# Group norms' deviation by ScalarE's logarithm and exponential in place of VectorE and GpSimd's power

## The chip, the cores and the metric

The kernel runs on one core of a Trainium2 chip. The metric is the device time of one execution in microseconds; the time of a kernel is the median of its runs. The engines are named as the profile names them: PE (TensorE's matmuls), PEld (its weight loads), DVE (VectorE), ACT (ScalarE), POOL (GpSimd) and SP (SyncE, which issues DMAs).

## The reference

Four layers work on 16 images of 192 channels and 32 x 32 pixels, all in fp32. Each layer is a residual around a block that sees the group-normalised image:

```python
def _gn(v, G=32, eps=1e-5):
    B_, C_, H_, W_ = v.shape
    g = v.reshape(B_, G, C_ // G, H_, W_)
    m = jnp.mean(g, axis=(2, 3, 4), keepdims=True)
    s = jnp.var(g, axis=(2, 3, 4), keepdims=True)
    return ((g - m) / jnp.sqrt(s + eps)).reshape(v.shape)

x = x + _L0_conv_ref(_gn(x), ...)   # layer norm, up projection, mLSTM over 1024 tokens, 3x3 conv, batch norm
x = x + _L1_conv_ref(_gn(x), ...)   # layer norm, selective scan (16 states, 384 channels), projection
x = x + _L2_conv_ref(_gn(x), ...)   # depthwise 3x3 conv, batch norm
x = x + _L3_conv_ref(_gn(x), ...)   # projection, depthwise conv, four selective scans, layer norm, router
return x
```

What matters here is `1 / sqrt(s + eps)` in `_gn`: one number for each of 32 groups, in each of 16 images and four layers.

## The kernel before, in words

An image lies in SBUF as 96 partitions x 2 halves of the channels x 1024 pixels. A group of six channels is six neighbouring partitions, so `group_norm` takes each partition's mean and variance on DVE (`bn_stats` L351, `bn_aggr` L352), averages over the six partitions with a small matmul against the constant `group` (L355, PSUM tile `mm`), builds the second moment on DVE (`gnmean` L357, `gnd` L359, `gnq` L361 and L362), and averages that with a second matmul (L365). The result in PSUM is the variance of the group, two columns for the two halves of the channels. DVE adds eps while it moves it to the SBUF tile `gnr` (L367), and `pow_mhalf` raises that in place to the power of -0.5 on GpSimd (L309). The caller then normalises the two halves on DVE, each a `tensor_scalar` over 96 x 1024 that reads `gnmean` and `gnr`:

- L543 in `layer0_image` (layer 0, 16 images), which `layer0_front`'s layer norm reads with the matmul L377;
- L1240 in `layer1_front` (layer 1), read likewise by L377;
- L1351 in `layer1_tail` (the norm ahead of layer 2), which fills `xpad`, sent to DRAM by L1356;
- L1545 in `layer3_front` (layer 3), which fills `xpad` too. There `router` also reads `gnr` on DVE (L1680).

The kernel runs in three stages: layer 0, then layers 1 and 2 together, then layer 3. Each has a main chain, and beside it tasks that a small planner (`Side`) interleaves: a task is a Python generator, added with a start and an end in units of main steps, and at each tick the planner draws as many of its pieces as are due. `group_norm` is part of such tasks (`image`, `front`, `tail`). The order in which instructions are written is then handed to the tile framework, which schedules each engine's queue by its own estimates and inserts the semaphores; instructions of one engine run in the order of its queue.

In layer 0 the main chain works through chunks of 128 tokens (`layer0_step`). GpSimd adds the mask and the row to the decay matrix `e`, 128 x 1536 (L705, L706), scales `hs` by `mhv` (L841), forms `vr` (L755) and adds `ht` (L857); ACT takes the exponential of `e` (L711); ACT takes a logarithm and an exponential of the small tile `mhv` (L839, L840); DVE multiplies `ht` (L854) ahead of L543.

In layers 1 to 3 the main chain is a selective scan (`scan_run`): per state n and unit of 512 tokens, ACT scales `xbt` (three L966) and forms the decay `da` (L986, five buffers) for each of three channel tiles, PE turns `xbt` into the PSUM tile `xb` (L994, and L997 with the diagonal made by GpSimd's L976), DVE scans (L1010, `h`), GpSimd copies the carry (L1016) and multiplies `h` by the row `cb` (L1017, 128 x 1536), and PE adds the result up in PSUM (L1028). ACT and PE work one to two steps ahead of the scan.

`layer_norm` already forms its deviation with AF.Ln and AF.Exp (L386, L387). Silu needs another table of ACT; after each Silu the kernel loads the set `natural_log_exp_and_others` again (L598, L1284). `batch_norm` and `layer3_weights` also call `pow_mhalf`; they are not touched.

Of the kernel before, what the change touches and what calls it, by code (L numbers as in the profile page):

```python
# [11 lines left out]
AF = mybir.ActivationFunctionType  # L12
# [4 lines left out]
ADD, SUB, MUL, MAX, MIN, POW = ALU.add, ALU.subtract, ALU.mult, ALU.max, ALU.min, ALU.pow  # L17

C = 192
HP = 96  # L20
# [8 lines left out]
EPS = 1e-5  # L29
# [160 lines left out]
def halves(n=S, step=512):  # L190
    return [slice(i, i + step) for i in range(0, n, step)]
# [83 lines left out]
class Program:  # L275
# [68 lines left out]
    def group_norm(self, pool, psum, x):  # L344

        nc = self.nc
        st = pool.tile([HP, 2, 2, 6], F32, name="gnst")
        mv = pool.tile([HP, 2, 2], F32, name="gnmv")
        for m in range(2):
            for i, h in enumerate(halves()):  # L350
                nc.vector.bn_stats(st[:, m, i], x[:, m, h])  # L351
            nc.vector.bn_aggr(mv[:, m], st[:, m].rearrange("p a b -> p (a b)"))  # L352
            yield 1
        ps = psum.tile([128, 512], F32, name="mm")
        nc.tensor.matmul(ps[:HP, :2], self.k("group", HP), mv[:, :, 0], start=True, stop=True)  # L355
        mean = pool.tile([HP, 2], F32, name="gnmean")
        nc.vector.tensor_copy(mean, ps[:HP, :2])  # L357
        d = pool.tile([HP, 2], F32, name="gnd")
        nc.vector.tensor_tensor(d, mv[:, :, 0], mean, SUB)  # L359
        q = pool.tile([HP, 2], F32, name="gnq")  # L360
        nc.vector.tensor_tensor(q, d, d, MUL)  # L361
        nc.vector.tensor_tensor(q, q, mv[:, :, 1], ADD)  # L362
        yield 1
        ps = psum.tile([128, 512], F32, name="mm")
        nc.tensor.matmul(ps[:HP, :2], self.k("group", HP), q, start=True, stop=True)  # L365
        r = pool.tile([HP, 2], F32, name="gnr")
        nc.vector.tensor_scalar(r, ps[:HP, :2], EPS, None, ADD)  # L367
        self.pow_mhalf(r)
        yield 1
        return mean, r, d  # L370

# [1339 lines left out]
```

## Time and profile before

| What | Value |
|---|---|
| Median of three runs | 17368.59 us (17350.56 to 17390.61) |
| Profiled execution | 17403.5 us, span 17401.7 us |
| Mean granted clock of TensorE | 0.951 |
| GpSimd's product L1017 | 2560 times, 3469 ns |
| DVE's scan L1010 | 7680 times, 1202 to 1262 ns |
| ACT's decay L986 and scaling L966 | 7680 times each, 714 and 603 ns |
| DVE's normalisations (96 x 1024) | 128 times, 0.79 us at least, 4.70 us at most |

The profile is of one execution, which has its own time; the table gives it beside its span, which runs from the first instruction to the last. In the profile's lines `out<-in` names tiles, `x` counts instructions, and a bracket or "idle before" gives the time in which the engine stood idle ahead of an instruction and what ended it. In the answers on a tile, three durations are the smallest, the median and the largest in ns; indented lines give idle time in us and how often. In the timeline the first column is the start in us from the span's start and the second how long the row took.

### The profile page before, as it was taken

How to read it: one execution, taken by the hardware profiler on the slowest of the kernel's cores; microseconds unless marked ns; L12 is line 12 of the kernel's file. 1: busy time of each engine (PE TensorE's matmuls, PEld its weight loads, DVE VectorE, ACT ScalarE, POOL GpSimd, SP SyncE). 2: the span in 40 equal slices, each digit the busy share in tenths (PEclk: the TensorE clock that was granted, in tenths of full speed). 3: DMA queues.
4: the chain of work that ended last, by engine and by line, in shares of the span. 5: the costliest groups of instructions: out<-in, count | busy, mean ns of one | idle time of the engine just before them, and what ended most of it. 6: DMA issues, size and time to landing. Idle time of an engine off the chain costs nothing. (4 is left out here: it accounts for less than half of the span.)

```text
span 17401.7 us, 263068 instructions
## 1 busy us (share of the span) xinstructions
PE 15749.6 (91%) x99452; PEld 11013.2 (63%) x99452; DVE 13122.0 (75%) x14859; ACT 11873.6 (68%) x19637; POOL 11450.8 (66%) x5555
## 2 busy tenths in 40 slices
PE   8998988888988899979899999999999999999998
PEld 4444444435555555547777777777777777777777
DVE  4444444437777777749889888888888888888888
ACT  3222322327666666648888888888888888888888
POOL 3333333425555555538788788888878888888888
PEclk8889998989999999989999999999999999999999
DMA  1111111123333343433333333323333333333332
GB/s 51 42 40 44 44 43 44 47 63 107 114 110 110 113 118 116 118 99 103 90 99 107 93 96 101 107 83 99 107 98 92 99 108 88 96 105 102 88 98 67
DMA packets 890141, 1544.65 MB, mean 89 GB/s; under 512 B 83472, under 2 KB 314653, under 8 KB 879530
## 3 DMA queue, kind: packets, MB, share of 16 engines
q1 hardware_dynamic: 888874, 1527.81, 30.3%
q8 instruction: 788, 12.91, 0.3%
q14 instruction: 479, 3.92, 0.1%
HBM read 1284.22 MB, written 243.27 MB: 88 GB/s over the span
## 5 line engine op out<-in xcount | busy, mean ns | idle before, releaser
L1017 POOL TENSOR_TENSOR h<-h,cb 128x1536 f32<-128x1536 f32 x2560 | 8872.8, 3469 | 1432.0 <-DVE h L1010 902.9
L986 ACT ACTIVATE da<-dt,neg_a 128x512 f32<-128x512 f32 x7680 | 5267.0, 714 | 1752.0 <-DVE h L1010 1687.3
L1010 DVE TENSOR_TENSOR_SCAN h<-da,carry,xb 128x512 f32<-128x512 f32 x3840 | 4652.4, 1262 | 657.1 <-PE xb L997 596.2
L1028 PE MATMUL y<-const,h 128*128 128x128 f32 x30720 | 4717.9, 276 | 128.3 <-DVE ysum L1468 54.0
L1010 DVE TENSOR_TENSOR_SCAN h<-da,xb 128x512 f32<-128x512 f32 x3840 | 4440.6, 1202 | 388.7 <-PE xb L997 270.7
L994 PE MATMUL xb<-const,xbt 128*128 128x128 f32 x23040 | 4074.6, 282 | 422.5 <-DVE h L1010 269.3
L966 ACT ACTIVATE xbt<-ut,bt 128x384 f32<-128x384 f32 x7680 | 4174.4, 603 | 246.4 <-PE xb L994 244.3
L994 PEld LDWEIGHTS xb<-const,xbt 128*128 128x128 f32 x23040 | 2757.2, 143 | 1815.5 <-issue 643.8
L1028 PEld LDWEIGHTS y<-const,h 128*128 128x128 f32 x30720 | 3684.9, 143 | 322.8 <-issue 265.4
L997 PE MATMUL xb<-diag,ut 128*128 128x128 f32 x15360 | 3016.4, 279 | 0.0
L997 PEld LDWEIGHTS xb<-diag,ut 128*128 128x128 f32 x15360 | 2383.5, 195 | 63.1 <-issue 63.1
L830 POOL TENSOR_TENSOR hs<-h,mhm 128x384 f32<-128x384 f32 x128 | 108.5, 848 | 1685.1 <-DVE den L835 1290.5
L1016 POOL COPY carry<-h 128x3 f32<-128x3 f32 x1280 | 250.5, 196 | 1220.1 <-DVE h L1010 964.7
L976 POOL TENSOR_TENSOR diag<-const,bt 128x512 f32<-128x512 f32 x640 | 680.8, 1064 | 550.5 <-PE xb L997 362.1
L705 POOL TENSOR_TENSOR e<-e,const 128x1536 f32<-128x1536 f32 x128 | 439.9, 3437 | 288.9 <-DMA e<-row 273.0
L520 PE MATMUL conv<-ya,w_conv 128*64 128x512 f32 (+1 forms) x1152 | 543.9, 656 | 66.1 <-DMA ya<-yrows 62.2
L916 PE MATMUL mm<-dbl,w_dt 45*128 45x512 f32 x960 | 532.8, 639 | 33.6 <-DVE v L1490 16.2
L711 ACT ACTIVATE e<-e 128x1536 f32<-128x1536 f32 x128 | 189.7, 1482 | 417.7 <-POOL e L706 417.4
L854 DVE TENSOR_TENSOR ht<-sz,mm 128x384 f32<-128x384 f32 x128 | 70.7, 552 | 519.5 <-PE mm L851 519.5
L1171 PE MATMUL mm<-rep,t_dw 96*32 96x512 f32 x2304 | 433.5, 614 | 23.5 <-DMA rep<-xr 17.3
L779 PEld LDWEIGHTS num<-v,p 128*128 128x128 f32 x3072 | 389.3, 201 | 102.2 <-issue 77.9
L920 DVE SCALAR_TENSOR_TENSOR dt<-lnsq,mm 128x512 f32<-128x512 f32 x480 | 322.0, 671 | 171.9 <-ACT lnsq L919 171.9
(272 smaller groups left out, 17910.1 us busy)
## 6 DMA issues: line engine op xcount, KB each, us to landing
cb<-row SPq DMA_DIRECT2D x2560, 256.0 KB
rep<-xr SPq DMA_DIRECT2D x384, 331.0 KB
e<-row SPq DMA_DIRECT2D x128, 768.0 KB
rep<-xin SPq DMA_DIRECT2D x384, 256.0 KB
rep<-xr SPq DMA_DIRECT2D x384, 228.8 KB
x<-x SPq DMA_DIRECT2D x48, 768.0 KB
xr<-xin SPq DMA_DIRECT2D x48, 612.5 KB
xr<-xpad SPq DMA_DIRECT2D x32, 867.0 KB
```

What stands on the lines that cost most here:

```text
L520: nc.tensor.matmul(o, self.w_c2[:k, t, c0 : c0 + o.shape[0]], src[:k, r0 : r0 + 16, dx : dx + W], start=t == 0, stop=t == 14, skip_group_c ...
L705: nc.gpsimd.tensor_tensor(k.e, k.e, self.k0("mask")[:, None, :].to_broadcast([128, NH, 128]), ADD)
L916: nc.tensor.matmul(ps, w_dt[:, t * 128 : (t + 1) * 128], dbl, start=True, stop=True)
L966: nc.scalar.activation(t[:, c], u.ut[:, c], AF.Copy, scale=u.bt[:, c, n : n + 1])
L976: nc.gpsimd.tensor_tensor(d, ident[:, None, :].to_broadcast([128, 4, 128]), u.bt[:, 3, n : n + 4][:, :, None].to_broadcast([128, 4, 128]), ...
L986: nc.scalar.activation(da[i, t], u.dt[:, t], AF.Exp, scale=u.neg_a(t, n))
L994: in_order(nc.tensor.transpose(xb[i, t][:, c * 128 : (c + 1) * 128], xbt[i][:, c, t * 128 : (t + 1) * 128], ident))
L997: in_order(nc.tensor.matmul(xb[i, t][:, 384:], u.ut[:, 3, t * 128 : (t + 1) * 128], u.diag[n // 4][:, n % 4], start=True, stop=True, skip_ ...
L1010: nc.vector.tensor_tensor_scan(hv, dv, xv, 0.0 if first else u.carry_in[:, n, t : t + 1], MUL, ADD)
L1017: nc.gpsimd.tensor_tensor(h[i], h[i], u.c.pop(n)[:, None, :].to_broadcast([128, 3, 512]), MUL)
L1028: in_order(nc.tensor.matmul(u.y[:, j], h[i][:, t, c * 128 : (c + 1) * 128], ident, is_transpose=True, start=n == 0 and j % 4 == 0, stop=n ...
L1171: self.nc.tensor.matmul(ps[32 * g : 32 * g + 32], blocks[:, g * side + r], seen, start=r == 0, stop=r == side - 1, skip_group_check=True,)
```

## The change

The add of eps moves into the bias of a logarithm on ACT, which reads the variance from PSUM and writes `gnr`; an exponential with scale -0.5 then forms the deviation in place, also on ACT. DVE's L367 and the call of `pow_mhalf` go.

```diff
         ps = psum.tile([128, 512], F32, name="mm")
         nc.tensor.matmul(ps[:HP, :2], self.k("group", HP), q, start=True, stop=True)
         r = pool.tile([HP, 2], F32, name="gnr")
-        nc.vector.tensor_scalar(r, ps[:HP, :2], EPS, None, ADD)
-        self.pow_mhalf(r)
+        nc.scalar.activation(r, ps[:HP, :2], AF.Ln, bias=self.k("eps", HP))
+        nc.scalar.activation(r, r, AF.Exp, scale=-0.5)
         yield 1
         return mean, r, d
```

Line numbers stay the same: in the changed kernel L367 is the logarithm and L368 the exponential. The framework schedules anew, so other instructions move a little too. In layer 0 the order stays as it was but for the first images. In layers 1 and 2 PE's, ACT's and DVE's queues have neighbours exchanged around the norms of every image: L1240 stands one scan earlier in DVE's queue, L1351 stands ahead of the scan that it followed. In layer 3 L1545 stands one scan later (a scan that followed it now precedes it), L1680 is followed by one more scan before the copy L1683, and one of SP's loads of `xtok` an image changes place. In ACT's queue the logarithm and the exponential follow L840 in layer 0, and stand among the L966 and L986 of the scan in the other layers.

## The prediction

> **What bounds the kernel now.** First the page's busy time, then the busy time by layer (layer 0; layers 1 and 2; layer 3), each row with PE, PEld, DVE, ACT, POOL and the granted clock.
>
> ```profile
> PE 15749.6 (91%) x99452; PEld 11013.2 (63%) x99452; DVE 13122.0 (75%) x14859; ACT 11873.6 (68%) x19637; POOL 11450.8 (66%) x5555
> ```
> ```profile
> 0.00:3860.00 3860.00, 3401.76 (x14460) 1725.32 (x14460) 1801.98 (x3622) 1110.81 (x1656) 1435.47 (x890) 0.88 0.18 44
> 3860.00:7660.00 3800.00, 3341.98 (x19456) 2167.84 (x19456) 2784.72 (x3055) 2508.77 (x4001) 2110.81 (x1033) 0.96 0.38 112
> 7660.00:17402.00 9742.00, 9005.87 (x65536) 7120.08 (x65536) 8535.31 (x8184) 8254.07 (x13980) 7904.54 (x3632) 0.97 0.33 97
> ```
>
> PE is near its bound everywhere, but its queue is in order, so it also stands still where it meets a late operand: 458 us in layer 0, 458 in layers 1 and 2, 736 in layer 3. The change can only win or lose inside that idle time. Next the answers for the tile gnr (first and third group below) and for the matmul L377, which reads the normalised image.
>
> ```profile
> L367 DVE TENSOR_SCALAR gnr<-mm x64: 122/145/156, 33.5 to 16416.9; 96x2 f32<-96x2 f32 x64
> L309 POOL TENSOR_TENSOR gnr<-gnr,const x64: 679/690/709, 33.7 to 16417.9; 96x2 f32<-96x2 f32 x64
> ...
>   POOL gnr L309: 95.0, 52
> ```
> ```profile
>   DVE x L543: 222.3, 45
> ...
>   DVE xf L1240: 72.3, 46
> ```
>
> The power takes 0.69 us, and VectorE sits idle 95.0 us in all for it, because it queues behind GpSimd's 3.4 us products. PE and its weight loads wait long for the normalisation itself (L543, L1240), of which the power is only the last link. Last, the timeline at one norm of each kind. Layer 0:
>
> ```profile
> 2759.37 2.75 POOL L706 TENSOR_TENSOR e<-e,uw 128x1536 f32<-128x1536 f32 x1
> 2762.08 0.69 POOL L309 TENSOR_TENSOR gnr<-gnr,const 96x2 f32<-96x2 f32 x1
> ...
> 2762.80 3.80 DVE L543 TENSOR_SCALAR x<-x,gnmean,gnr 96x1024 f32<-96x1024 f32 x2 [5.33 <-POOL gnr L309]
> ...
> 2765.93 3.73 PE L377 MATMUL mm<-x,const 96*96 96x512 f32 x4 [7.05 <-DVE x L543]
> ```
>
> Layer 1's tail (L1351) and layer 3 (L1545):
>
> ```profile
> 5226.79 0.69 POOL L309 TENSOR_TENSOR gnr<-gnr,const 96x2 f32<-96x2 f32 x1 [2.19 <-DVE gnr L367]
> ...
> 5227.82 4.64 DVE L1351 TENSOR_SCALAR xpad<-xt,gnmean,gnr 96x1024 f32<-96x1024 f32 x2
> ...
> 5228.03 3.88 POOL L1017 TENSOR_TENSOR h<-h,cb 128x1536 f32<-128x1536 f32 x1 [0.56 <-DVE h L1010]
> ```
> ```profile
> 10992.26 1.61 ACT L966 ACTIVATE xbt<-ut,bt 128x384 f32<-128x384 f32 x3
> ...
> 10995.36 0.25 PE L365 MATMUL mm<-gnq,const 96*96 96x2 f32 x2
> ...
> 10997.56 0.71 POOL L309 TENSOR_TENSOR gnr<-gnr,const 96x2 f32<-96x2 f32 x1
> ...
> 10998.31 2.24 DVE L1545 TENSOR_SCALAR xpad<-x,gnmean,gnr 96x1024 f32<-96x1024 f32 x2 [1.62 <-POOL gnr L309]
> ```
>
> A pair of normalisations takes 1.6 us alone and up to 4.64 beside a GpSimd product: who comes first at that moment matters more than the power's own 0.69 us.
>
> [...] L1351 takes 0.79 us alone and 3.94 when L1017 got in before it. [...] The trace: 204 ns for the 96x2 exponential L1690, 212 for the 128x12 logarithm L839. [...] the order of the changed kernel agrees, with 228 table loads where there were 227, the new one in the first microseconds (1.28 us).
>
> **The change part by part.** It removes 64 L367 (64 x 0.145 = 9.3 us of VectorE) and 64 powers (64 x 0.69 = 44 us of GpSimd) and adds 64 logarithms [...] and 64 exponentials (0.20): 31 us of ScalarE. None of these sums is the effect; the places are. No DMA is added; some of SP's issues swap places with a neighbour (one xtok load an image in layer 3, a few replicas in layer 1). I cost those at nothing: the loads' reader is far off.
>
> *Layer 0.* VectorE's order is unchanged but for L367, ScalarE has the pair right after L840. L711, next behind it, starts at 2762.15 and is not touched. At 2756.28 + 0.21 + 0.48 = 2757.0 the deviation is there, 5.8 us before L543 starts now. But GpSimd is in L705 and L706 until 2762.12[...]. Between L706, L841, L755 and L857 there is no gap, so the second half of L543 waits for L857 (end 2765.33) as now, 0.7 us sooner since the power is gone. L706 follows L705 after a gap of 0.08 us, and at 201.01 a half L543 slipped into just such a gap. So in the five norms of this form the first half goes at 2759.3, and half of L377 (3.73 / 2 = 1.9 us) is done before the second: 0.7 + 1.9 = 2.6 us. In nine others L706 is already running: 0.65. Sum 5 x 2.6 + 9 x 0.65 = 19 us off PE's wait; I keep three quarters, 14 us, as the next wait (for e, L711) takes some; bounds 9 and 19.
>
> *Layer 1, front (L1240), 13 steady norms.* ScalarE's logarithm stands one L966 earlier than its input allows: ScalarE waits from 5145.85 to PE's result at 5147.62, 1.8 us, with L966 (xbt) and three L986 (da) behind it. PE's tile needs that xbt at 5148.22 and gets it at 5148.5. VectorE reaches L1240 one scan (1.2 us) sooner, at 5148.85, in the middle of L1017 (to 5150.24) with L976 behind it: 2.4 us of waiting where there were 1.4, and L377 stands before the next L997 in PE's order. Worked through, the second scan after it ends at 5157.5 where it was 5157.15: a loss of 0.3 us, 4 us in all. Bounds: a gain of 1 us each (13)[...]; a loss of 2.5 (33), if PE's new order holds a scan back.
>
> *Layer 1, tail (L1351), 11 norms of the form shown.* ScalarE is idle when the matmul ends (5225.19); deviation at 5225.7. L1351 now stands ahead of the scan that releases L1017, so GpSimd is idle during both halves: 5226.57 to 5228.1, then the scan to 5229.3, where scan and pair were over at 5232.46. VectorE gains 3.1 us; PE's idle there is 1.57 <-DVE h plus 0.36 <-DVE gnr, so 1.9 us, 21 in all; I take three quarters, 16 (bounds 0, if other waits fill the place, and 3.1 x 11 = 34). L1017 comes about 1 us later; its reader is two steps off.
>
> *Layer 3 (L1545), 14 norms.* The logarithm stands between the first and second of the three L966: ScalarE waits from 10992.86 to 10995.6, 2.8 us. The third L966 ends at 10997.15 where PE asked for it at 10996.50 (0.65 us of PE, then idle anyway until 11001.73 <-DVE h); the next decay at 10997.8, its scan at 10999.9. VectorE does one scan more before L1545, arrives at 10997.7, in L976 (now from 10997.58 to 10998.62), and is done at 10999.95 where it was 11000.55 with a scan less: 1.16 + 0.6 = 1.7 us. L1680, now two scans earlier, meets L1017 sooner: about 1.2 us instead of 0.55. Net 1.0; 14 norms, less a little: 12 us. Bounds 0 and 24.
>
> Four norms with nothing beside them (the first of each layer and the last tail) go from 0.97 us between L367's start and the normalisation's to about 0.55: 1.6 us, which pays for the one table load. **Sum:** -14 + 4 - 16 - 12 = -38 us. The profiled execution took 17403.5 us (span 17401.7), 35 above the median of the three runs, so it gives 17365 for a like execution and 17330 against the median of 17368.6.
>
> **Rivals.**
> *Nothing comes of it* (17364): [...] (14 x 0.65 = 9, less L1240's 4). For it: PE at 88 to 92%. Against: PE's idle at these places is named <-DVE.
> *ScalarE's queue becomes the wait; slower.* Place: the logarithm ahead of L966 and L986 in L1240 and L1545. Price: 13 x 1.8 + 14 x 2.8 = 62 us; less layer 0's 14, 48 slower: 17417. It decides if the decays come later than the scans: they have 2.1 us to spare in layer 3 (10997.8 against 10999.9), and the five da buffers. Against: ScalarE's idle of 1752 us ahead of L986 is time in which it is ahead. For: it is 85% busy there.
> *More is gained* (17278): layer 0 19, L1351 3.1 x 11 = 34, L1545 1.7 x 14 = 24, L1240 13, sum 90.
> *It reloads tables* (each 1.28 us, 128 of them 164 us slower): excluded by the order.
>
> **Numbers.** About 0.2% (35 us) is what a measurement tells from no change. Forecast 17330: 0.50, spread on both sides of that line; nothing 0.20; more 0.12; slower 0.18. Faster 0.45, same 0.38, slower 0.17. The range goes from the larger gain (17265) to the queue's loss with a little over for the unexamined reordering of PE in layers 1 and 2 (17430).
>
> **What would show it.** VectorE's wait for gnr gone and L543's first half longer than 3.1 us in layer 0; L1351 at 0.8 us in both halves; L1545 still near 1.5 then 0.8; ScalarE idle about 2.8 us at each L367 <-PE mm L365. Wrong if L986 or L966 becomes a long releaser of PE or VectorE, if L1351 still shows 3.9, or if layer 3 is not shorter.

## The result and the profile after

The changed kernel takes 17282.36 us (median of 4 runs, 17259.77 to 17310.99) where the kernel before takes 17367.28 in the same session; the ratio is 0.9951, with a 95% interval of 0.9932 to 0.9970. That is a gain of 85 us, with an interval of 52 to 118. A second session with the same kernel gave 17266.54 against 17356.26, ratio 0.9946 (0.9933 to 0.9960). The forecast was a gain of 38 us: the direction was right, and the time lies in the range, near its faster end, but the gain is more than twice the forecast. The profiled execution took 17310.99 us (span 17309.2), which is 29 us above the median.

The page's busy time, and then the stretches of layer 0, of layers 1 and 2 and of layer 3 (duration, then PE, PEld, DVE, ACT, POOL with the number of instructions, the granted clock, the DMA share and GB/s):

```profile
PE 15753.3 (91%) x99452; PEld 11004.9 (64%) x99452; DVE 13120.8 (76%) x14795; ACT 11898.1 (69%) x19766; POOL 11425.1 (66%) x5491
```
```profile
0.00:3826.00 3826.00, 3414.34 (x14460) 1731.56 (x14460) 1819.66 (x3607) 1117.82 (x1689) 1436.29 (x874) 0.88 0.18 45
3826.00:7577.00 3751.00, 3345.51 (x19456) 2175.33 (x19456) 2757.42 (x3018) 2523.20 (x4064) 2084.65 (x1001) 0.96 0.38 114
7577.00:17310.00 9733.00, 8993.41 (x65536) 7098.04 (x65536) 8543.70 (x8171) 8257.12 (x14014) 7904.15 (x3616) 0.98 0.31 97
```

No engine's total moved by more than 26 us, and TensorE is as busy as it was (15753 us against 15750). What shrank is the time in which it stands: in layer 0 from 458 to 412 us, in layers 1 and 2 from 458 to 405. In layer 3 it is 740 where it was 736. The gain thus shows where the forecast placed 26 us in all, and does not show, in this pair of profiles, where it placed 12.

The groups of the tile gnr, and the answer for the matmul L377:

```profile
L367 ACT ACTIVATE gnr<-mm,const x64: 240/258/260, 36.0 to 16330.2; 96x2 f32<-96x2 f32 x64
L368 ACT ACTIVATE gnr<-gnr x64: 188/198/204, 37.6 to 16330.9; 96x2 f32<-96x2 f32 x64
...
  PE mm L365: 156.8, 48
  ACT gnr L368: 9.7, 13
```
```profile
  DVE x L543: 134.5, 51
...
  DVE xf L1240: 52.6, 57
```

VectorE no longer waits 95.0 us for GpSimd's power; it waits 9.7 us for the exponential. ScalarE stands 156.8 us in all before the logarithm, 3.3 us each of 48 times. TensorE and its weight loads wait 88 us less for L543 and 20 us less for L1240. Now the same three places as in the prediction. Layer 0:

```profile
2726.30 3.11 DVE L838 SCALAR_TENSOR_TENSOR mhv<-mhv,den 128x12 f32<-128x12 f32 x1
...
2729.46 2.75 POOL L706 TENSOR_TENSOR e<-e,uw 128x1536 f32<-128x1536 f32 x1
2729.80 0.24 ACT L367 ACTIVATE gnr<-mm,const 96x2 f32<-96x2 f32 x1
2730.08 0.20 ACT L368 ACTIVATE gnr<-gnr 96x2 f32<-96x2 f32 x1
2730.32 3.68 DVE L543 TENSOR_SCALAR x<-x,gnmean,gnr 96x1024 f32<-96x1024 f32 x2 [0.44 <-ACT gnr L368]
2732.17 1.28 POOL L841 TENSOR_TENSOR hs<-hs,mhv 128x384 f32<-128x384 f32 x1
...
2732.81 3.73 PE L377 MATMUL mm<-x,const 96*96 96x512 f32 x4 [4.41 <-DVE x L543]
```

L543 is issued in the middle of L706 and its first half ends 0.55 us after L706 does (2732.76 against 2732.21), although L841 follows L706 without a gap. Its second half waits for L841 and ends 0.55 us after it (2734.00 against 2733.45); neither half waits for L755 or L857. In the kernel before the first half ended 3.76 us after the end of L706.

Eight of the 13 norms from the fourth on have this form in the changed kernel's profile. In the other five L838, which ScalarE's L839 and L840 and the pair behind them wait for, takes 0.16 us where it takes 3.11 above, beside L705. There the deviation is ready while L705 runs, the first half of L543 gets in between L705 and L706 and ends 0.55 us after L705, and the second waits for L706 and ends 0.55 us after it:

```profile
2028.88 0.16 DVE L838 SCALAR_TENSOR_TENSOR mhv<-mhv,den 128x12 f32<-128x12 f32 x1
2028.88 3.45 POOL L705 TENSOR_TENSOR e<-e,const 128x1536 f32<-128x1536 f32 x1 [2.21 <-DMA e<-row]
...
2030.43 5.62 DVE L543 TENSOR_SCALAR x<-x,gnmean,gnr 96x1024 f32<-96x1024 f32 x2
2032.42 3.08 POOL L706 TENSOR_TENSOR e<-e,uw 128x1536 f32<-128x1536 f32 x1
2032.94 2.02 PE L377 MATMUL mm<-x,const 96*96 96x512 f32 x2 [1.02 <-DVE x L543]
```

Layer 1's tail and layer 3:

```profile
5181.02 0.26 ACT L367 ACTIVATE gnr<-mm,const 96x2 f32<-96x2 f32 x1 [2.21 <-PE mm L365]
...
5182.35 1.53 DVE L1351 TENSOR_SCALAR xpad<-xt,gnmean,gnr 96x1024 f32<-96x1024 f32 x2
5183.80 1.27 DVE L1010 TENSOR_TENSOR_SCAN h<-da,carry,xb 128x512 f32<-128x512 f32 x1
...
5185.20 3.47 POOL L1017 TENSOR_TENSOR h<-h,cb 128x1536 f32<-128x1536 f32 x1 [4.82 <-DVE h L1010]
```
```profile
10906.73 0.26 ACT L367 ACTIVATE gnr<-mm,const 96x2 f32<-96x2 f32 x1 [2.52 <-PE mm L365]
...
10909.03 2.21 DVE L1545 TENSOR_SCALAR xpad<-x,gnmean,gnr 96x1024 f32<-96x1024 f32 x2
...
10913.40 1.17 DVE L1680 TENSOR_TENSOR xm<-gnd,gnr 96x2 f32<-96x2 f32 x1
```

L1351's pair takes 1.53 us where it took 4.64, ahead of the scan that lets L1017 start. In layer 3 the pair takes 2.21 us where it took 2.24 and L1680 takes 1.17 us, as the prediction had it.

### The profile page after: what moved, and what is told of

It reads as the page before. It is cut to its first block, busy times and chain, and to the rows that moved or that the text cites. A ratio compares the mean times of both kernels' runs of the same rounds, so it can differ in the third digit from the quotient of the medians.

```text
span 17309.2 us, 262978 instructions
## 1 busy us (share of the span) xinstructions
PE 15753.3 (91%) x99452; PEld 11004.9 (64%) x99452; DVE 13120.8 (76%) x14795; ACT 11898.1 (69%) x19766; POOL 11425.1 (66%) x5491
## 5 line engine op out<-in xcount | busy, mean ns | idle before, releaser
L1017 POOL TENSOR_TENSOR h<-h,cb 128x1536 f32<-128x1536 f32 x2560 | 8871.6, 3469 | 1454.9 <-DVE h L1010 978.7
L986 ACT ACTIVATE da<-dt,neg_a 128x512 f32<-128x512 f32 x7680 | 5267.5, 714 | 1612.7 <-DVE h L1010 1556.7
L1010 DVE TENSOR_TENSOR_SCAN h<-da,carry,xb 128x512 f32<-128x512 f32 x3840 | 4653.3, 1263 | 706.4 <-PE xb L997 655.0
L1010 DVE TENSOR_TENSOR_SCAN h<-da,xb 128x512 f32<-128x512 f32 x3840 | 4440.6, 1202 | 391.8 <-PE xb L997 271.0
L966 ACT ACTIVATE xbt<-ut,bt 128x384 f32<-128x384 f32 x7680 | 4174.7, 603 | 204.7 <-PE xb L994 203.0
L705 POOL TENSOR_TENSOR e<-e,const 128x1536 f32<-128x1536 f32 x128 | 440.4, 3440 | 272.6 <-DMA e<-row 255.1
```

The source lines that it names most:

```text
L705: nc.gpsimd.tensor_tensor(k.e, k.e, self.k0("mask")[:, None, :].to_broadcast([128, NH, 128]), ADD)
L966: nc.scalar.activation(t[:, c], u.ut[:, c], AF.Copy, scale=u.bt[:, c, n : n + 1])
L986: nc.scalar.activation(da[i, t], u.dt[:, t], AF.Exp, scale=u.neg_a(t, n))
L1010: nc.vector.tensor_tensor_scan(hv, dv, xv, 0.0 if first else u.carry_in[:, n, t : t + 1], MUL, ADD)
L1017: nc.gpsimd.tensor_tensor(h[i], h[i], u.c.pop(n)[:, None, :].to_broadcast([128, 3, 512]), MUL)
```

## The experiments

### Which of the four places gains (e1 to e4)

The helper gets a switch, and one place at a time uses it; the others keep addition and power. Against the kernel before:

```
-    def group_norm(self, pool, psum, x):
+    def group_norm(self, pool, psum, x, on_act):
...
-        nc.vector.tensor_scalar(r, ps[:HP, :2], EPS, None, ADD)
-        self.pow_mhalf(r)
+        if on_act:
+            nc.scalar.activation(r, ps[:HP, :2], AF.Ln, bias=self.k("eps", HP))
+            nc.scalar.activation(r, r, AF.Exp, scale=-0.5)
+        else:
+            nc.vector.tensor_scalar(r, ps[:HP, :2], EPS, None, ADD)
+            self.pow_mhalf(r)
```

e1_layer0:

> The changed kernel with Ln and Exp in the norms of layer 0 alone (L543 of the changed kernel, 14 norms); the norms of layers 1 and 3 keep the addition on VectorE and the power on GpSimd. Theory (each place has its own mechanism; here the first half of L543 comes early enough to fill the gap before L377): the whole gain of layer 0, which the two profiles put at 34 us (the batch norm of layer 1 ends at 3836.8 before and 3802.8 after), so some 17333 us, and nothing in layers 1 and 3. Rival (every norm gains the same, whatever runs beside it, from the time that VectorE and GpSimd no longer spend on addition and power: 85 us over 52 norms, 1.6 us each): 14 x 1.6 = 23, so 17344 us. The prediction on record had 14 us for this place (17353).

e2_front1:

> Ln and Exp in the front norms of layer 1 alone (L1240, 13 norms), power everywhere else. Theory: the front norm is worth the fall of TensorE's idle time before L377 that ends with L1240, 30.6 to 18.4 us, so about 12 us (17355 us), and what else the layer gained belongs to its other norm. Rival (same gain at every norm): 13 x 1.6 = 21 us (17346). The prediction on record had a loss of 4 us here (17371).

e3_tail1:

> Ln and Exp in the tail norms of layer 1 alone (L1351, 11 norms), power everywhere else. Theory ([...] the scale comes 3 us earlier, so both halves of L1351 run ahead of the scan that releases GpSimd's L1017[...]): the second half of L1351 takes 0.8 us instead of 3.9 in nearly all norms, TensorE's idle time before L994 in layers 1 and 2 falls from 48 towards 16 us, and the kernel gains about 34 us (17333). Rival (same gain at every norm): 11 x 1.6 = 18 us (17349). The prediction on record had 16 us (17351).

e4_layer3:

> Ln and Exp in the norms of layer 3 alone (L1545, 14 norms), power everywhere else. Theory (each norm gains 1.0 us where it stands, and loses it some 15 scans later, where TensorE pauses for 2.5 us at the router's operations and then runs at half clock for several us): a gain of 0 to 7 us (17360 to 17367), the mean time of one image of layer 3 stays 602 us. Prediction on record: 12 us (17355). Rival (same gain at every norm): 14 x 1.6 = 23 us (17344).

The four ran on one chip, the kernel before at 17357.67 us. The gains are worked out from the ratios and their intervals, the forecast's own terms beside them:

| place | median us | ratio (95%) | gain us (95%) | forecast us |
|---|---|---|---|---|
| layer 0, L543 | 17321.00 | 0.9977 (0.9970 to 0.9985) | 40 (26 to 52) | 14 |
| layer 1 front, L1240 | 17356.28 | 1.0000 (0.9992 to 1.0008) | 0 (-14 to 14) | -4 |
| layer 1 tail, L1351 | 17320.63 | 0.9976 (0.9969 to 0.9982) | 42 (31 to 54) | 16 |
| layer 3, L1545 | 17345.36 | 0.9994 (0.9986 to 1.0002) | 10 (-3 to 24) | 12 |

The parts add up to 92 us, the whole change gave 85; within the intervals nothing is lost or won by having them together. The even gain of 1.6 us a norm is out: L1240 with 13 norms gains nothing, L1351 with 11 gains 42. My own figure of 12 us for L1240, read from the fall of one wait, is near the end of its interval and is not borne out.

A warning on reading stages from single profiles came with these runs. Layer 0 is the same code in the kernel before and in e2, e3 and e4, and it took 3863.8, 3860.6, 3851.2 and 3829.6 us there. The 34 us that the first two profiles seemed to show for layer 0 is no more than this scatter; the gain rests on the repeated runs. The scatter goes with the clock: added up from the traces' clock records, TensorE was at half clock in that stretch for 931, 921, 892 and 867 us, in the same order.

What happens at each norm is steadier than the stages. I took TensorE's matmuls of layer 0 in both traces, matched them one to one, and compared how far e1 is ahead of the kernel before shortly ahead of each norm and shortly after it: from the fourth norm on, e1 gains 3.2 to 3.9 us at every one, 46 us over 13. The addition and the power that it no longer has are 0.15 and 0.69 us, so at most 11 us over 13 norms. In the changed kernel's profile the eight norms of the first form gain 2.6 to 3.8 us and the five of the second 4.0 to 4.6. For L1351 the scans L1010 matched in the same way (from 4 scans ahead of the norm to 25 scans after) show 3.4 to 3.7 us at each of the 11 norms of that form. One such stretch, the same 197 matmuls, in the kernel before and then in e3_tail1 (columns as above):

```profile
5226.00:5262.00 36.00, 32.87 (x197) 17.63 (x195) 27.19 (x27) 27.35 (x41) 19.41 (x7) 1.00 0.62 178
```
```profile
5201.82:5234.40 32.58, 32.09 (x197) 18.00 (x195) 23.71 (x26) 27.43 (x41) 18.33 (x6) 1.00 0.69 197
```

The stretch is 3.42 us shorter, TensorE's idle time in it falls from 3.13 to 0.49 us, and VectorE is busy 3.48 us less, most of it the 3.1 us that it no longer stands in L1351.

### Is it the place or the removed instructions (b_early0, b_ahead, a_behind, e5_idle_pow)

The first three hold an instruction behind another on its own engine's queue, by an added order without a wait. b_early0 keeps every power; from the fourth image of layer 0 on, L706 is held behind the power, and L841 and L755 (late) behind L706:

```
+        ins = self.pow_mhalf(r)
+        if early:
+            self.power = ins.ins.name
...
+            self.follows(ins, self.power)
...
+            for late in self.late.values():
+                self.follows(late, ins.ins.name)
```

> The kernel before, its addition on VectorE and its power on GpSimd kept in all 64 norms; in 13 norms of layer 0 GpSimd's queue alone is changed: the power stands between L705 and L706 (numbers of the kernel before) in place of behind L706, and L841 and L755 stay behind L706. Theory (what counts is that the deviation is there before L706 ends, so that [...] half of L377 runs 2 to 3 us earlier): most of what the logarithm gains in this layer comes without it, 13 x 3.0 less 13 x 0.7 for the exponential e that now comes one power later, about 30 us, bounds 15 and 40, from 17357 to some 17327. Rival (the gain is the time of the removed instructions): nothing is removed here, so no gain, or 13 x 0.7 = 9 us slower (17366).

It took 17323.97 us against 17362.81, ratio 0.9979 (0.9972 to 0.9986): a gain of 36 us (24 to 49) with all powers in place. An order alone, with nothing removed, gains about what the logarithm gains in layer 0; the rival is out. But more than the power's place was turned: on GpSimd L867 (L857 before) now runs ahead of L763 (L755 before), VectorE's L864, which L867 waits for, stands between the halves of the normalisation, and a few neighbours on ScalarE and TensorE changed places. So the 36 us is not the price of the power's place alone. The timeline shows that the mechanism is not quite the one expected:

```profile
1360.89 0.69 POOL L309 TENSOR_TENSOR gnr<-gnr,const 96x2 f32<-96x2 f32 x1
1361.54 2.75 POOL L709 TENSOR_TENSOR e<-e,uw 128x1536 f32<-128x1536 f32 x1
1361.61 4.02 DVE L546 TENSOR_SCALAR x<-x,gnmean,gnr 96x1024 f32<-96x1024 f32 x1 [3.91 <-POOL gnr L309]
1364.25 0.83 POOL L850 TENSOR_TENSOR hs<-hs,mhv 128x384 f32<-128x384 f32 x1
...
1365.68 2.02 PE L379 MATMUL mm<-x,const 96*96 96x512 f32 x2 [6.47 <-DVE x L546]
...
1366.17 1.50 POOL L867 TENSOR_TENSOR ht<-ht,xact 128x384 f32<-128x384 f32 x1 [1.09 <-DVE ht L864]
```

(L709, L850, L546 and L379 are here what L706, L841, L543 and L377 are in the kernel before.) The normalisation waits for L709 and for L850 behind it, 4.02 us, and still comes 4.70 us after the end of L708 (1365.63 against 1360.93), where L543 came 6.59 us after the end of the same product before. In e1 it came 3.38 us after. A longer wait, begun earlier, ends earlier. Here it ended behind L850, after which GpSimd stood idle for 1.09 us.

b_ahead and a_behind turn the order at L1351. In b_ahead, made from the kernel before, the next third scan L1010 of a group is held behind L1351; in a_behind, made from the changed kernel, L1351 is planned 0.9 steps later and held behind the last scan planned ahead of it:

```
b_ahead:
+            if t == 2 and getattr(self, "norm", None):
+                self.follows(ins, self.norm)
a_behind:
+        yield Wait(0.9)
...
+                self.follows(ins, self.scanned)
```

> The kernel before, power kept in all norms; on VectorE's queue the scan that releases GpSimd's L1017 is held behind both halves of L1351, in every tail norm of layer 1. Theory [...]: both halves of L1351 at 0.8 us with no logarithm at all; the pair starts 1.0 us later than in the changed kernel because the power is still there, so 2.1 of the 3.1 us a norm, 11 x 2.1 = 23 us, up to 28, so 17330 to 17335. Rival (the gain comes from the power's and the addition's own 0.8 us on the chain): nothing is gained (17357), or the held scan costs 1 us a norm (17368).

> The changed kernel with logarithm and exponential in all norms, but L1351 is held on VectorE's queue behind the scan that releases L1017, where it stood before. Theory [...]: the second half of L1351 is back at 3.9 us and what the tail norms gained is lost, 30 to 42 us, so 17303 to 17315 where the changed kernel is at 17273 on this chip (85 below the kernel before). Rival (the earlier deviation is what counts): it stays within 10 us of the changed kernel, 17273 to 17283.

b_ahead: 17346.94 against 17362.81, ratio 0.9990 (0.9982 to 0.9998), a gain of 17 us (3 to 31), the lower side of what was expected. a_behind: 17308.21, ratio 0.9973 (0.9962 to 0.9985), so 47 us of the 85 are left (26 to 66) and about 38 are gone. The groups of L1351 (min, median and max in ns), first b_ahead, then a_behind:

```profile
L1359 DVE TENSOR_SCALAR xpad<-xt,gnmean,gnr x32: 786/807/811, 4273.2 to 7528.8; 96x1024 f32<-96x1024 f32 x32
```
```profile
L1357 DVE TENSOR_SCALAR xpad<-xt,gnmean,gnr x32: 783/798/3956, 4237.0 to 7516.3; 96x1024 f32<-96x1024 f32 x32
```

With the power still there but the order turned, no half ever takes more than 0.811 us; with the logarithm but the old order, 12 of the second halves take 3.9 us. The matched scans, from 4 ahead of the norm to 25 after, give the shares: at the 11 norms b_ahead gains 1.1 to 2.0 us, e3_tail1 3.4 to 3.7, and a_behind nothing (within 0.1 us at nine of them, 0.7 and 1.4 us slower at two). So without the order this place gains nothing, and the order alone, with the power still there, gains somewhat over a third: VectorE then stands 0.80 us ahead of each pair, with the scan held behind it. The rest comes with the earlier deviation, which brings L1351 to VectorE in time for that order. The 0.9 steps by which a_behind plans L1351 later were not tested apart from its order.

e5_idle_pow spends GpSimd's time again:

```
+        junk = pool.tile([HP, 2], F32, name="gnjunk")
+        nc.gpsimd.tensor_tensor(junk, r, self.k("mhalf", HP)[:, :2], POW)
```

> The changed kernel, and besides it a power on GpSimd in each of the 64 norms, into a tile that nobody reads: the 44 us of GpSimd's time that the change saved are spent again, off the path to the normalisation. Theory (place and moment count, not GpSimd's time): the gain stays, 70 to 85 us, so 17273 to 17288. Rival (GpSimd's saved time is the gain): half of it goes, 40 us or more, so 17313 or above.

It took 17293.00 us, ratio 0.9962 (0.9948 to 0.9976): 66 us faster than the kernel before (42 to 90). That is a little below the 70 to 85 us expected. Most of the gain stays, so GpSimd's time is not its main source; that some 19 us of the 85 come from it, the interval leaves open, and its lower end, 42 us, just touches what the rival allowed.

### Layer 3: what is gained and what is lost again (a_pointer, b_pointer, a_columns, after_again)

The forecast for layer 3 held, 12 us against 10 (-3 to 24), but the interval holds nothing too. So I matched layer 3's scans L1010 with those of the kernel before, in every kernel, from 4 scans ahead of each of the 14 norms. The sums over the norms, in us (minus is faster):

| kernel | 10 scans after | 40 scans after |
|---|---|---|
| power in layer 3: e1, e2, e3, b_early0, b_ahead | -0.9 to 0.4 | -3.5 to 1.8 |
| logarithm in layer 3: changed kernel, after_again, e4, a_behind, e5 | -16.3 to -12.4 | 3.6, -1.3, -8.9, -5.9, -7.6 |

In each kernel that has the logarithm there, a norm gains 0.8 to 1.6 us (two kernels' first norm excepted, which gains nothing); with power the difference stays within 0.6 us. Some 15 scans later, at the router, steps of 3.3 us take much of it back, at up to six of the 14 norms. Such steps come with the power too, up to two a kernel and in both directions (b_ahead has one each way). One of these in the changed kernel, and the same place in the kernel before:

```profile
10329.00:10336.00 7.00, 7.00 (x32) 4.58 (x27) 3.95 (x4) 4.08 (x7) 4.70 (x2) 0.51 0.18 64
```
```profile
10422.30:10427.50 5.20, 5.20 (x43) 3.75 (x44) 4.74 (x5) 4.24 (x8) 4.76 (x3) 1.00 0.19 72
```

Both start at the same work. TensorE is busy throughout in both, but at a granted clock of 0.51 it gets through 32 matmuls in 7 us where it gets through 43 in 5.2 at full clock. Just ahead of it TensorE had stood 2.02 and 2.52 us, the second time <-DVE h; in the kernel before these were 2.07 and 0.86, with 3.41 us at half clock soon after the first (from 10414.83). In the changed kernel's clock records 103 of the 226 stretches at half clock last 3.41 us and 78 last 6.83, and all but one of the 226 are a multiple of 3.41 long; the one here lasts 6.83 (from 10329.02). What starts such a stretch is not shown; that here it was two pauses near each other is my reading and was not tested alone.

The 2.52 us come from VectorE, which stands behind GpSimd's L1017 in tiny operations of the router: ahead of this pause L1563, 96x2, takes 2.39 us and ends 0.02 us after L1017. a_pointer and b_pointer write three of them with per-partition scalars:

```
-        nc.vector.tensor_tensor(xm, d, r, MUL)
-        nc.vector.tensor_tensor(top, e[:, 0:1], e[:, 1:2], MAX)
-        nc.vector.scalar_tensor_tensor(wb, self.v96("3pw_b", 0, 2), wts[:, 1:2], wb, MUL, ADD)
...
+        nc.vector.tensor_scalar(xm[:, m : m + 1], d[:, m : m + 1], r[:, m : m + 1], None, MUL)     # m = 0, 1
+        nc.vector.tensor_scalar(top, e[:, 0:1], e[:, 1:2], None, MAX)
+        nc.vector.tensor_scalar(wb[:, m : m + 1], self.v96("3pw_b", m), wts[:, 1:2], wb[:, m : m + 1], MUL, ADD)
```

> The changed kernel with three small VectorE operations of layer 3's router written with per-partition scalars in place of second tensors: L1688 (2.38 us each, in the changed kernel, though it is 96x1), L1563 (2.39 us) and L1680 (0.5 to 1.7 us) become tensor_scalar, as L1689 and L1562 beside them already are (0.22 us). Theory (in layer 3 VectorE stands behind GpSimd's L1017 at these operations, TensorE pauses some 2.5 us for it once an image and part of the norm's gain is lost there): 0.9 to 2.5 us an image of 14, so 12 to 35 us more than the changed kernel: 85 + 12 to 85 + 35 below the kernel before on this chip (17240 to 17263 if that is at 17360). Rival (VectorE's scans wait for TensorE there, so its stalls are covered): the same as the changed kernel, 17275, within 10 us.

> The same three operations rewritten in the kernel before, addition and power kept. Theory (the same stalls are there, TensorE pauses 0.9 us): 12 to 20 us faster than the kernel before (17340 to 17348 if that is at 17360), and less than the rewriting gives in the changed kernel, where the pause is longer. Rival (stalls covered): no difference, within 10 us.

a_pointer: 17253.36 against 17360.19, ratio 0.9936 (0.9922 to 0.9950), a gain of 111 us (87 to 135); that is 26 more than the change alone, but the intervals overlap. b_pointer: 17363.36, ratio 1.0002 (0.9994 to 1.0011), nothing; the 12 to 20 us expected there did not come. In both the stall had moved to the next operation of two columns, as a_pointer's group shows beside that of the kernel before (its L1563):

```profile
L1562 DVE TENSOR_SCALAR wb<-p,re x16: 224/2299/2306, 7676.6 to 16297.6; 96x2 f32<-96x2 f32 x16
```
```profile
L1563 DVE SCALAR_TENSOR_TENSOR wb<-p,re,wb x16: 192/2391/2526, 7789.7 to 16437.4; 96x2 f32<-96x2 f32 x16
```

a_columns takes the rest to one column each (L1562, L1689, L1693, and the sum L1691 as tensor_scalar):

```
-        nc.vector.tensor_scalar(e, e, top, None, SUB)
+        for m in range(2):
+            nc.vector.tensor_scalar(e[:, m : m + 1], e[:, m : m + 1], top, None, SUB)
...
```

> The changed kernel with all small VectorE operations of layer 3's router, L1562 and L1680 as tensor_scalar on one column (96x1) each. In a_pointer 80 operations of the kind 96x1 with per-partition scalars took 0.18 to 0.27 us without an exception, while the stall behind GpSimd's L1017 moved to the 96x2 operations left (L1562 2.3 us, L1691 1.15 us) and to the sum L1693 (up to 3.4 us). Theory [...]: none of these operations takes over 0.4 us, VectorE gets 3 us an image back, and 14 images give 10 to 30 us more than a_pointer: 17225 to 17245 where the kernel before is at 17360. Rival (what TensorE waits for there does not hang on these operations, or the stall goes on to the copy L1683 and the scans): within 10 us of a_pointer, 17245 to 17263.

> The changed kernel once more, unaltered, on the same chip as a_columns, so that the two are compared directly and layer 3 is seen in one more profile: 85 us below the kernel before, within its interval of 52 to 118. If layer 3 gains nothing, its part of the profile (from the first L1545 to the end) is again near the 9723 us of the six profiles with power there (9715 to 9735); if it gains the 12 us of the prediction, it lies near 9711, as in a_behind and e5_idle_pow.

a_columns: 17240.80 us (17229.08 to 17250.92) against 17356.26, ratio 0.9932 (0.9920 to 0.9945). after_again, beside it: 17266.54 (17255.74 to 17273.08). Every run of a_columns is below every run of the changed kernel; the medians differ by 26 us. This is the fastest version seen. The operation that stalled 2.3 us, now twice as many instructions:

```profile
L1563 DVE TENSOR_SCALAR wb<-p,re x32: 198/201/204, 7677.2 to 16286.2; 96x1 f32<-96x1 f32 x32
```

In the matched scans a_columns is 45.3 us ahead of the kernel before 10 scans after the norms and still 33.8 ahead 40 scans after; a_pointer had 43.1 and 11.2. Against a_pointer, in another session, a_columns gains 13 us by the medians and 7 by the ratios, which the rival (within 10 us) allows too: a gain over a_pointer alone is not shown.

How the stalls and the clock hang together is seen in the time that TensorE spends at half clock around the 14 norms, added up from the clock records (us):

| kernel | 4 scans ahead to 10 after | 10 to 25 after |
|---|---|---|
| power in layer 3, six profiles | 92 to 106 | 29 to 36 |
| logarithm in layer 3, five profiles | 51 to 62 | 41 to 60 |
| b_pointer | 90 | 68 |
| a_pointer | 38 | 75 |
| a_columns | 53 | 36 |

b_pointer is 19 us ahead of the kernel before 10 scans after the norms and 9 us behind 25 scans after, in step with the 68 us. With the router's other small operations down to one column too, the 75 us of a_pointer are 36 in a_columns.

after_again puts layer 3 (first L1545 to the end of the engines' work) at 9716.1 us, between the two figures it was to tell apart. All kernels with the router unaltered together: 9715.4 to 9735.0, mean 9725, in six profiles with power, and 9701.4 to 9723.1, mean 9712, in five with the logarithm. The difference of 13 us agrees with the forecast, but the groups overlap. The time at half clock in that stretch does not: 458 to 492 us with power, 400 to 439 with the logarithm, 62 us less in the mean, which at half speed is worth at most 31 us of TensorE's work (an estimate from these sums). Around the norm the logarithm saves such time, at the router it loses some of it again.

## Why the prediction was right or wrong

**Where the gain sits.** Right in the main: in TensorE's waits for the normalisations, not in any engine's total, and the parts add up to the whole within the intervals. The two places that carry the gain were each forecast at less than half of it.

**Layer 0, 14 us forecast, 40 measured.** Two terms failed. The first is the wait for GpSimd: "Between L706, L841, L755 and L857 there is no gap, so the second half of L543 waits for L857 (end 2765.33) as now". In the kernel before it is the first half that waits for L857, issued when L841 has just begun (2762.80 against 2762.73), and the second takes 0.80 us:

```profile
2762.80 3.08 DVE L543 TENSOR_SCALAR x<-x,gnmean,gnr 96x1024 f32<-96x1024 f32 x1 [5.33 <-POOL gnr L309]
```

Issued while L705 or L706 runs, L543 gets in at the end of that product (its first half ends 0.55 us later), and neither half waits for L857. The split into five norms of 2.6 us and nine of 0.65 rested on that wait; e1 shows 3.2 to 3.9 us at 13 norms, all with L543 issued inside L706. The sign to look for, a first half longer than 3.1 us, was wrong for the same reason: it takes 2.44 to 2.94. The second is the moment of the deviation. "At 2756.28 + 0.21 + 0.48 = 2757.0 the deviation is there" took over the moment of L838 from the kernel before, where it took 0.16 us at this image:

```profile
2755.84 0.16 DVE L838 SCALAR_TENSOR_TENSOR mhv<-mhv,den 128x12 f32<-128x12 f32 x1
```

In the changed kernel L838 takes 3.11 us there, and the logarithm, behind it in ScalarE's order, starts 0.34 us after L706 (2729.80 against 2729.46). The deviation that is ready during L705, with the first half in the gap ahead of L706, did come at five other norms.

**Layer 1's tail, 16 us forecast, 42 measured.** The mechanism was right, and b_ahead and a_behind show it. The term "PE's idle there is 1.57 <-DVE h plus 0.36 <-DVE gnr, so 1.9 us" was too small, for it stopped at TensorE's first waits. TensorE's idle time in the stretch falls by 2.64 us, since a third wait of 0.71 us follows at 5238.62 of the kernel before, and the stretch shortens by 3.42. VectorE's whole 3.1 us came through. The quarter that I took off was not lost, and the upper bound of 34 us lies low in the measured interval of 31 to 54.

**Layer 1's front, a loss of 4 us forecast, 0 measured (14 either way).** Not contradicted. Its halves take 2.08 and 1.52 us where they took 1.51 and 0.80, so VectorE does meet L1017 at a worse moment, as forecast. In e2_front1 the matched scans stand 0.3 to 2.9 us later 10 scans after 12 of the 13 norms (8.1 at the other), more than the 0.3 us forecast; 25 scans after, the sum over the norms is 6 us earlier, no different from the 1 to 9 of kernels that keep the power there.

**Layer 3, a gain of 12 us forecast, 10 measured (-3 to 24).** The local term of 1.0 us is right to a few tenths, and yet the agreement is in part luck. That the gain stays to the end was assumed; the matched scans show that much of it is lost at the router within 40 scans. And the forecast has no term for the clock, while the time at half clock changed by 62 us in this layer, for the better at the norm and for the worse at the router. How much remains of the local gain, and how much of it is the clock's, is open.

**The rivals.** ScalarE's queue did not become the bound: it stands 156.8 us before the logarithm, and TensorE's waits in layer 3 for xbt (L966) went from 86.1 to 90.3 us only. The rival of a larger gain was near in its sum (90), and wrong in its parts: it had 19 us in layer 0, 24 in layer 3 and 13 at L1240. Nor are tables reloaded: the trace has 228 loads of 1.283 us where there were 227, of them 224 around Silu (L596, L598, L1283, L1284) in both. The price of the logarithm, 0.28 us, was my estimate, and no row of the kernel before shows it; in the trace it is 0.258 us, and 0.198 for the exponential, so 0.46 for the pair where 0.48 was forecast.

## What to carry to other kernels

Here a VectorE operation was priced by what GpSimd was running when it was issued: a half of L543 took 0.80 us with nothing beside it, 2.44 issued 0.86 us into L706, and 3.08 issued 0.07 us into L841. So a small change of its start was worth microseconds: ask what it will meet at the new moment, and don't carry over the wait of the old one. Where the engine that stalls feeds the one that bounds, count its whole gain until a later wait has been shown to take it back, and follow the chain beyond the first wait. A local gain isn't a gain yet: b_pointer's 19 us were gone 25 scans later. A pause of TensorE may cost more than its length through the clock: the pauses of 2.02 and 2.52 us above were followed by 6.83 us at half clock, though what set that off was not tested. Tiny operations that cause such pauses are worth rewriting together: three of them alone gained nothing in the kernel before.

## What the hardware showed

**One column did not wait here.** Beside GpSimd's L1017, a tensor_scalar of 96x2 took up to 2.31 us (L1562 in a_pointer), and a tensor_scalar of 96x1 never did: the 32 of L1563 in a_columns lie between 198 and 204 ns, and with up to two per-partition scalars none in a_pointer or a_columns took over 0.271 us. With two tensors as inputs one column was not enough: L1688, a tensor_tensor of 96x1 with both inputs in SBUF, takes 2.38 to 2.39 us in 14 of its 16 cases in the changed kernel, and each of these ends 0.01 to 0.02 us after L1017. Why the form makes the difference was not shown.

**When GpSimd lets go.** Between two GpSimd instructions that follow each other without a gap the traces show both outcomes: VectorE came in between L706 and L841 in the changed kernel, and did not in b_early0, nor between L841, L755 and L857 in the kernel before. Over the 13 norms from the fourth on, in the kernel before, in the changed kernel and in b_early0, every half that waited ends 0.55 us after the GpSimd instruction that it waited for. The 26 that had to wait for further instructions (kernel before and b_early0) were issued 0.06 to 0.07 us after the start of one on GpSimd; the 26 that got in at the end of the running one (changed kernel) 0.4 us or more after its start. Whether this decides it was not tested.
